# Masks on GpSimd, gelus in place in PSUM and a pair loop in a fixed issue order

## The chip, the cores and the metric

The kernel runs on one core of a Trainium2 chip. The metric is the device time of one execution, in microseconds, and lower is better. Engines are named as the profile names them: PE (TensorE matmuls), DVE (VectorE), ACT (ScalarE), POOL (GpSimd), SP (the queue that issues most transfers). PSUM is the on-chip memory into which the matmuls of this kernel write, SBUF the one that holds its other tiles. A "round" below is one step of the loop over pairs of nodes, normally 128 x 1024 elements.

## The reference, cut to what matters

Two graph layers on 3327 nodes with 64 features. The first is a hyperbolic attention over all pairs of nodes, weighted by an adjacency matrix of zeros and ones. The second sums, for each node, its last hundred neighbours with weights that halve from one to the next, so it needs a count of the later neighbours of each pair.

```python
adj_att = sigmoid(left[:, None] + right[None, :] + b) * adj          # layer 0
support_t = einsum('ij,ijd->id', adj_att, logmap(x[:, None], x[None, :]))
...
mask = (adj != 0)                                                    # layer 1
rank = cumsum(mask, axis=1); deg = rank[:, -1:]
k = minimum(deg, 100); pos = rank - (deg - k)
out = (mask * where(pos > 0, 0.5 ** (k - pos), 0)) @ support + bias
```

## The kernel before

The pair loop goes through four strips of columns (1024, 1024, 768 and 512 wide). Strips 0 to 2 have 26 rounds each; the last handles two row blocks a round and has 13. In each round VectorE makes a mask from the adjacency tile, PE adds it to a running count in PSUM (`pc`), ScalarE or VectorE copies the count out; ScalarE makes a tanh and two gelus, VectorE two large products, and PE sums the result (`po`). Between the rounds of a strip some 90 small VectorE and ScalarE operations finish the strip before (`steps`).

```python
ad = work.tile([P, FMAX], F32, name="ad", bufs=4)                       # adjacency
mask = work.tile([P, FMAX], BF16, name="mask", bufs=3)
V.tensor_scalar(mask[:, :span], ad[:, :span], 0.0, None, op0=ALU.not_equal)
for j in js:
    ...  # T.matmul(pc, ca, before); T.matmul(pc, cb, now)               count
    if j % (2 if b0 == 0 else 4):
        A.activation(kept, pc[:, :F], AF.Relu)                          # count read
    else:
        V.tensor_scalar(kept, pc[:, :F], 0.0, None, op0=ALU.max)
for j in js:
    A.activation(part(sg, j), left_b[:, :F], AF.Tanh, bias=right[:, j : j + 1], scale=0.5)
V.scalar_tensor_tensor(sg, sg, 1.0, ad, op0=ALU.add, op1=ALU.mult)      # first product
pq = ps.tile([P, FMAX], F32, name="pq", bufs=2)                         # pair buffer
...  # four matmuls into pq                                             products
A.activation(s, pq, AF.Gelu, scale=-WG / QS)                            # to SBUF
A.activation(s, s, AF.Gelu, scale=WH)
V.scalar_tensor_tensor(s, s, WD, sg, op0=ALU.add, op1=ALU.mult)         # second product
...  # T.matmul(po, hw, s)                                              total
next(steps, None)
```

The compiler's scheduler may reorder instructions within each engine's queue.

## Time and profile before

| what | before |
|---|---|
| time, median of 3 runs | 460.64 us (459.14 to 461.43) |
| busy PE / DVE / ACT / POOL | 378 / 407 / 369 / 13 us of 459 |
| loop, by the copies that end its strips | 48 to 143.3, 247.3, 330.3 and 390.3 us |
| last stage | 390.3 to 459.1 us |

A busy share says how much of a stretch an engine was occupied. Two more rows of the page, the gelus of the kernel before (operation, shape, count; busy time and mean ns; idle time before them and what ended it):

```profile
L851 ACT ACTIVATE s<-s 128x1024 f32<-128x1024 f32 (+1 forms) x91 | 91.4, 1006 | 0.1
L850 ACT ACTIVATE s<-pq 128x1024 f32<-128x1024 f32 (+1 forms) x91 | 87.7, 969 | 2.6 <-PE pq L848 2.6
```

The first gelu waits for PE only 2.6 us in all: its pair buffer is nearly always ready.

### The profile page before, as it was taken

How to read it: one execution, taken by the hardware profiler on the slowest of the kernel's cores; microseconds unless marked ns; L12 is line 12 of the kernel's file. 1: busy time of each engine (PE TensorE's matmuls, PEld its weight loads, DVE VectorE, ACT ScalarE, POOL GpSimd, SP SyncE). 2: the span in 40 equal slices, each digit the busy share in tenths (PEclk: the TensorE clock that was granted, in tenths of full speed). 3: DMA queues.
4: the chain of work that ended last, by engine and by line, in shares of the span. 5: the costliest groups of instructions: out<-in, count | busy, mean ns of one | idle time of the engine just before them, and what ended most of it. 6: DMA issues, size and time to landing. Idle time of an engine off the chain costs nothing.

```text
span 459.1 us, 4660 instructions
## 1 busy us (share of the span) xinstructions
PE 378.4 (82%) x1484; PEld 153.4 (33%) x1484; DVE 407.1 (89%) x774; ACT 369.2 (80%) x423; POOL 13.3 (3%) x30
## 2 busy tenths in 40 slices
PE   0266699999989799999997999889778897699293
PEld 0035233333323233333333444434322332244152
DVE  3895689999988999999998999999999998999821
ACT  1445989999894999999995999999599995888310
POOL 6000000000000000001000000020000000000000
PEclk9997699999999999999999999999999998899877
DMA  7103354545541444444442444344533420000003
GB/s 201 62 1 72 105 168 143 141 151 163 167 135 46 133 143 140 137 137 137 137 127 75 136 137 140 106 128 125 168 93 111 121 89 1 1 1 1 0 0 82
DMA packets 22840, 47.77 MB, mean 104 GB/s; under 512 B 8652, under 2 KB 9082, under 8 KB 22808
## 3 DMA queue, kind: packets, MB, share of 16 engines
q1 hardware_dynamic: 20522, 46.47, 34.7%
q10 hardware_dynamic: 2062, 0.87, 0.9%
q0 software_dynamic: 224, 0.07, 0.3%
q8 instruction: 13, 0.21, 0.2%
q14 instruction: 19, 0.16, 0.1%
HBM read 45.22 MB, written 0.85 MB: 100 GB/s over the span
## 4 chain that ended last, share of the span: by engine, by line

## 5 line engine op out<-in xcount | busy, mean ns | idle before, releaser
L855 PE MATMUL po<-s,hw 128*65 128x512 f32 (+1 forms) x364 | 165.3, 576 | 11.5 <-DVE s L852 11.1
L842 DVE SCALAR_TENSOR_TENSOR sg<-sg,ad 128x1024 f32<-128x1024 f32 (+1 forms) x91 | 103.5, 1141 | 7.5 <-ACT sg L841 7.3
L852 DVE SCALAR_TENSOR_TENSOR s<-s,sg 128x1024 f32<-128x1024 f32 (+1 forms) x91 | 104.8, 1152 | 3.7 <-ACT s L851 3.6
L841 ACT ACTIVATE sg<-left_b,right 128x1024 f32<-128x1024 f32 (+2 forms) x104 | 102.7, 1001 | 0.1
L851 ACT ACTIVATE s<-s 128x1024 f32<-128x1024 f32 (+1 forms) x91 | 91.4, 1006 | 0.1
L850 ACT ACTIVATE s<-pq 128x1024 f32<-128x1024 f32 (+1 forms) x91 | 87.7, 969 | 2.6 <-PE pq L848 2.6
L829 PE MATMUL pc<-mask,ca 128*128 128x512 bf16 (+1 forms) x175 | 65.7, 375 | 17.3 <-DVE behind_hi L836 7.2
L855 PEld LDWEIGHTS po<-s,hw 128*65 128x65 f32 x364 | 45.2, 138 | 98.9 <-issue 52.7
L847 PE MATMUL pq<-iu,ju 71*128 71x512 f16 (+1 forms) x182 | 67.8, 374 | 11.6 <-ACT s L850 11.6
L830 PE MATMUL pc<-mask,cb 128*128 128x512 bf16 (+1 forms) x182 | 66.7, 376 | 5.3 <-DVE mask L824 5.1
L848 PE MATMUL pq<-iz,jz 128*128 128x512 f16 (+1 forms) x182 | 66.6, 371 | 0.0
L824 DVE TENSOR_SCALAR mask<-ad 128x1024 bf16<-128x1024 f32 (+1 forms) x91 | 59.3, 654 | 3.4 <-PE pc L829 1.8
L894 PE MATMUL pw<-wt,s 128*128 128x512 bf16 (+1 forms) x182 | 41.0, 390 | 12.9 <-DVE s L782 9.2
L834 ACT ACTIVATE behind_hi<-pc 128x1024 uint8<-128x1024 f32 (+2 forms) x37 | 31.8, 860 | 24.3 <-PE pc L830 24.1
L830 PEld LDWEIGHTS <-cb 128*128 128x128 bf16 x182 | 17.9, 99 | 57.8 <-issue 46.6
L834 ACT ACTIVATE behind_lo<-pc 128x1024 uint8<-128x1024 f32 (+2 forms) x33 | 28.2, 853 | 7.1 <-PE pc L830 6.4
L894 PEld LDWEIGHTS <-s 128*128 128x128 f16 x182 | 18.7, 103 | 35.0 <-DVE s L782 9.6
L848 PEld LDWEIGHTS <-jz 128*128 128x128 f16 x182 | 18.1, 99 | 31.5 <-issue 15.3
L829 PEld LDWEIGHTS <-ca 128*128 128x128 bf16 x175 | 17.5, 100 | 30.8 <-issue 19.5
L847 PEld LDWEIGHTS <-ju 71*128 71x128 f16 x182 | 18.1, 100 | 21.4 <-issue 4.8
L836 DVE TENSOR_SCALAR behind_lo<-pc 128x1024 uint8<-128x1024 f32 (+2 forms) x19 | 19.9, 1050 | 1.1 <-PE pc L830 1.1
L771 POOL TENSOR_TENSOR x_sb<-x_sb,bias_b 128x512 f32<-128x512 f32 (+2 forms) x4 | 6.3, 1577 | 418.4 <-DVE w L769 418.4
(209 smaller groups left out, 290.0 us busy)
## 6 DMA issues: line engine op xcount, KB each, us to landing
ad<-in_adj_t SPq DMA_DIRECT2D x65, 512.0 KB, 3.7
ad<-in_adj_t SPq DMA_DIRECT2D x26, 384.0 KB, 3.3
out<-o SPq DMA_DIRECT2D x6, 128.0 KB, 2.0
x_sb<-in_x SPq DMA_DIRECT2D x1, 416.0 KB
x_sb<-in_x ACTq DMA_DIRECT2D x1, 416.0 KB, 6.9
iz<-jz ACTq DMA_DIRECT2D x2, 128.0 KB
iz<-jz SPq DMA_DIRECT2D x2, 128.0 KB, 2.4
iz<-jz SPq DMA_DIRECT2D x2, 96.0 KB
```

The costliest lines, as they stand in the source:

```text
L829: T.matmul(pc[:, f0:f1], ca, before[:, f0:f1], start=False, stop=True, skip_group_check=True)
L830: T.matmul(pc[:, f0:f1], cb, now[:, f0:f1], start=False, stop=True, skip_group_check=True)
L834: A.activation(kept, pc[:, :F], AF.Relu)
L841: A.activation(part(sg, j), left_b[:, :F], AF.Tanh, bias=right[:, j : j + 1], scale=0.5)
L842: V.scalar_tensor_tensor(sg[:, :span], sg[:, :span], 1.0, ad[:, :span], op0=ALU.add, op1=ALU.mult)
L847: T.matmul(part(pq, j, f0, f1), ju[:KB, j, :], iuf[:, f0:f1], start=True, stop=False)
L848: T.matmul(part(pq, j, f0, f1), jz[:, j, :], izf[:, f0:f1], start=False, stop=True)
L850: A.activation(s[:, :span], pq[:, :span], AF.Gelu, scale=-WG / QS)
L851: A.activation(s[:, :span], s[:, :span], AF.Gelu, scale=WH)
L852: V.scalar_tensor_tensor(s[:, :span], s[:, :span], WD, sg[:, :span], op0=ALU.add, op1=ALU.mult)
L855: T.matmul(po[: D + 1, f0:f1], hw[:, j, :], part(s, j, f0, f1), start=j == NB - 1, stop=j == 0)
L894: T.matmul(pw[n], s2[:, j].rearrange("p c d -> p (c d)"), wt[:, f0:f1].bitcast(BF16), start=j == 0, stop=j == NB - 1)
```

## The change

Its intent is to take the masks from the fullest engine, to let the second product have only one SBUF input so that a mask on GpSimd can run beside it, and to write the loop as a software pipeline whose order on PE, VectorE and ScalarE is fixed. Cut to its core:

```diff
+AHEAD = 3
+ON_ACT = ((1, 6), (2, 5), (1, 2), (1, 2))       # share of count reads on ScalarE, by strip
...
+    def edges(n):
+        mask_of[n] = mask = work.tile([P, FMAX], BF16, name="mask", bufs=3)
+        made = G.tensor_scalar(mask[:, : span(n)], ad_of[n][:, : span(n)], 0.0, 0.0,
+                               op0=ALU.is_equal, op1=ALU.is_equal)
+        if n - AHEAD in sg_inst:                # released by the first product of n - 3
+            tc.add_manual_dep(made.ins, sg_inst[n - AHEAD].ins.name, ...)
...
+    with tc.manual_schedule(engines={DVE, Activation, PE}):
...      # for each round n, m = n + 3:
+            total(n - 1)
+            A.activation(pq[:, :w], pq[:, :w], AF.Gelu, scale=-WG / QS)
+            A.activation(pq[:, :w], pq[:, :w], AF.Gelu, scale=WH)
+            sg_inst[n] = V.scalar_tensor_tensor(sg, sg, 1.0, ad_of.pop(n), ...)   # first product
+            read()                              # VectorE's count read, round m - 1
+            edges(m)
+            if two: count(m, js(m)[0])          # last strip only; may read on ScalarE
+            products(n + 1); sigmoids(n + 1)
+            for _ in js(n): next(steps, None)
+            read()
+            count(m, js(m)[-1])                 # may read on ScalarE
+            V.scalar_tensor_tensor(sg, pq, WD, sg, ...)                           # second product
```

Besides, the count no longer starts from a rank-one matmul, later strips fetch `left_b` from memory instead of by transposes, strip changes are pipelined, and the range check's transposes move to the last stage.

More of the change, by code (lines that the diff above doesn't have):

```diff
@@ L31 @@
 JH = 13
+AHEAD = 3
+SGB = 4
+ON_ACT = ((1, 6), (2, 5), (1, 2), (1, 2))
 GSTRIPS = [(0, 7), (7, 7), (14, 6), (20, 6)]
@@ L67 @@
 HS = 1024.0
-CNT = 127.0
 def halves(n):
@@ L480, in fast @@
                     pattern=[[-1, P]], channel_multiplier=1)
-    G.affine_select(out=cb, in_=cb, compare_op=ALU.not_equal, fill=CNT, base=0,
+    G.affine_select(out=cb, in_=cb, compare_op=ALU.not_equal, fill=float(MAX_NEIGH), base=0,
                     pattern=[[-1, P]], channel_multiplier=1)
     G.tensor_sub(ca, ca, cb)
-    row1 = const.tile([1, P], BF16, name="row1")
-    G.memset(row1, 1.0)
-    rowc = const.tile([1, 512], BF16, name="rowc")
-    G.memset(rowc, MAX_NEIGH - CNT)
     node = const.tile([P, NB], F32, name="node")
@@ L526, in fast @@
     s2 = const.tile([P, NB, 2, D], F16, name="s2")
+    left_d = tc.dram_tile([NP], F32, name="left_d")
     post_pool = ctx.enter_context(tc.tile_pool(name="post", bufs=1))
@@ L636, in fast @@
         V.tensor_scalar(right, right, batt, 0.5, op0=ALU.add, op1=ALU.mult)
+        plt = ps.tile([P, P], F32, name="po")
+        T.transpose(plt[:NB, :], left, ident)
+        left_t = const.tile([NB, P], F32, name="left_t")
+        V.tensor_copy(left_t, plt[:NB, :])
+        nc.sync.dma_start(left_d.rearrange("(b p) -> b p", p=P), left_t)
         wn, opx = small("wn"), small("opx")
@@ L658, in behind, with range_steps @@
         return behind_lo[:, j] if j < JH else behind_hi[:, j - JH]
-    def in_range():
-        st = post_pool.tile([P, 4], F32, name="st")
+    def range_steps():
         t1 = post_pool.tile([P, NB], F32, name="st1")
@@ L665, in in_range @@
         V.tensor_reduce(st[:, 0:1], t1, AX.X, ALU.max)
+        yield
         V.scalar_tensor_tensor(t1, x2, c_c, t1, op0=ALU.mult, op1=ALU.mult)
         V.tensor_reduce(st[:, 1:2], t1, AX.X, ALU.max)
+        yield
         V.tensor_mul(t1, bal, node)
         V.tensor_reduce(st[:, 2:3], t1, AX.X, ALU.max)
+        yield
         V.tensor_reduce(st[:, 3:4], t1, AX.X, ALU.min)
         V.tensor_scalar(st[:, 3:4], st[:, 3:4], -1.0, None, op0=ALU.mult)
-        pf = ps.tile([P, P], F32, name="pq", bufs=2)
+    def in_range(pool):
+        pf = pool.tile([P, P], F32, name="pf")
         T.transpose(pf[:4, :], st, ident)
@@ L675, in in_range @@
         V.tensor_reduce(st2, pf[:4, :], AX.X, ALU.max)
-        pf = ps.tile([P, P], F32, name="pq", bufs=2)
+        pf = pool.tile([P, P], F32, name="pf")
         T.transpose(pf[:1, :4], st2, ident[:4, :4])
@@ L782, in post, with strip_in @@
         V.tensor_sub(s2[:, bs, 1], w, s2[:, bs, 0])
-    steps = iter(())
-    for b0, nb in STRIPS:
-        F = nb * P
-        i0 = b0 * P
-        hv = halves(F)
+    rounds = []
+    for k, (b0, nb) in enumerate(STRIPS):
+        per = FMAX // (nb * P)
+        rounds += [(k, max(hi - per, 0), hi) for hi in range(NB, 0, -per)]
+    R = len(rounds)
+    class Strip:
+        pass
+    strips = [Strip() for _ in STRIPS]
+    ad_of, mask_of, sg_of, pq_of, sg_inst = {}, {}, {}, {}, {}
+    reads = []
+    st = const.tile([P, 4], F32, name="st")
+    def strip_in(k):
+        S = strips[k]
+        b0, nb = STRIPS[k]
+        S.F, S.i0, S.hv, S.read, S.before, S.first = nb * P, b0 * P, halves(nb * P), 0, None, True
         blocks = slice(b0, b0 + nb)
-        queue = nc.scalar if b0 == 0 else nc.sync
+        queue = nc.scalar if k == 0 else nc.sync
         iz = strip.tile([P, 8, P], F16, name="iz")[:, :nb]
@@ L798, in fast @@
         queue.dma_start(iz[D:], jz[:D, blocks])
-        izf, iuf = iz.rearrange("p b q -> p (b q)"), iu.rearrange("p b q -> p (b q)")
-        pc = ps.tile([P, FMAX], F32, name="pc")
-        po = ps.tile([P, FMAX], F32, name="po")
-        pl = ps.tile([P, FMAX], F32, name="pq", bufs=2)
-        for b in range(nb):
-            T.transpose(pl[:, b * P : (b + 1) * P], left[:, b0 + b : b0 + b + 1].to_broadcast([P, P]), ident)
-        left_b = strip.tile([P, FMAX], F32, name="left_b", bufs=1)
-        A.copy(left_b[:, :F], pl[:, :F])
@@ L807, in fast @@
-        for f0, f1 in hv:
-            T.matmul(pc[:, f0:f1], row1, rowc[:, : f1 - f0], start=True, stop=True, skip_group_check=True)
-        per = FMAX // F
-        before = None
-        for hi in range(NB, 0, -per):
-            lo = max(hi - per, 0)
-            js = range(hi - 1, lo - 1, -1)
-            span = (hi - lo) * F
-            def part(t, j, a=0, b=F):
-                return t[:, (j - lo) * F + a : (j - lo) * F + b]
-            ad = work.tile([P, FMAX], F32, name="ad", bufs=4)
-            nc.sync.dma_start(ad[:, :span].rearrange("p (b f) -> p b f", f=F),
-                              adj_t[lo * P : hi * P, i0 : i0 + F].rearrange("(b p) f -> p b f", p=P))
-            mask = work.tile([P, FMAX], BF16, name="mask", bufs=3)
-            V.tensor_scalar(mask[:, :span], ad[:, :span], 0.0, None, op0=ALU.not_equal)
-            for j in js:
-                now = part(mask, j)
-                for f0, f1 in hv:
-                    if before is not None:
-                        T.matmul(pc[:, f0:f1], ca, before[:, f0:f1], start=False, stop=True, skip_group_check=True)
-                    T.matmul(pc[:, f0:f1], cb, now[:, f0:f1], start=False, stop=True, skip_group_check=True)
-                before = now
-                kept = behind(j)[:, i0 : i0 + F]
-                if j % (2 if b0 == 0 else 4):
-                    A.activation(kept, pc[:, :F], AF.Relu)
-                else:
-                    V.tensor_scalar(kept, pc[:, :F], 0.0, None, op0=ALU.max)
-            sg = work.tile([P, FMAX], F32, name="sg", bufs=3)
-            for j in js:
-                A.activation(part(sg, j), left_b[:, :F], AF.Tanh, bias=right[:, j : j + 1], scale=0.5)
-            V.scalar_tensor_tensor(sg[:, :span], sg[:, :span], 1.0, ad[:, :span], op0=ALU.add, op1=ALU.mult)
-            pq = ps.tile([P, FMAX], F32, name="pq", bufs=2)
-            for j in js:
-                for f0, f1 in hv:
-                    T.matmul(part(pq, j, f0, f1), ju[:KB, j, :], iuf[:, f0:f1], start=True, stop=False)
-                    T.matmul(part(pq, j, f0, f1), jz[:, j, :], izf[:, f0:f1], start=False, stop=True)
-            s = work.tile([P, FMAX], F32, name="s", bufs=3)
-            A.activation(s[:, :span], pq[:, :span], AF.Gelu, scale=-WG / QS)
-            A.activation(s[:, :span], s[:, :span], AF.Gelu, scale=WH)
-            V.scalar_tensor_tensor(s[:, :span], s[:, :span], WD, sg[:, :span], op0=ALU.add, op1=ALU.mult)
-            for j in js:
-                for f0, f1 in hv:
-                    T.matmul(po[: D + 1, f0:f1], hw[:, j, :], part(s, j, f0, f1), start=j == NB - 1, stop=j == 0)
-                next(steps, None)
@@ L857, in fast @@
-        for _ in steps:
-            pass
-        ot = work.tile([P, FMAX], F32, name="s", bufs=3)[: D + 1]
-        V.tensor_copy(ot[:, :F], po[: D + 1, :F])
-        pa = ps.tile([P, FMAX], F32, name="pq", bufs=2)
+        S.iz, S.iu = iz.rearrange("p b q -> p (b q)"), iu.rearrange("p b q -> p (b q)")
+        S.left = strip.tile([P, FMAX], F32, name="left_b")
+        if k == 0:
+            pl = ps.tile([P, FMAX], F32, name="pq", bufs=2)
+            for b in range(nb):
+                T.transpose(pl[:, b * P : (b + 1) * P], left[:, b0 + b : b0 + b + 1].to_broadcast([P, P]), ident)
+            A.copy(S.left[:, : S.F], pl[:, : S.F])
+        else:
+            nc.sync.dma_start(S.left[:, : S.F], bass.AP(tensor=left_d.tensor, offset=left_d.offset + S.i0,
+                                                         ap=[[0, P], [1, S.F]]))
@@ new lines, in part, with span, js, load @@
+    def part(n, t, j, a=0, b=None):
+        k, lo, hi = rounds[n]
+        F = strips[k].F
+        return t[:, (j - lo) * F + a : (j - lo) * F + (F if b is None else b)]
+    def span(n):
+        k, lo, hi = rounds[n]
+        return (hi - lo) * strips[k].F
+    def js(n):
+        k, lo, hi = rounds[n]
+        return range(hi - 1, lo - 1, -1)
+    def load(n):
+        k, lo, hi = rounds[n]
+        S = strips[k]
+        ad_of[n] = ad = work.tile([P, FMAX], F32, name="ad", bufs=AHEAD + 3)
+        nc.sync.dma_start(ad[:, : span(n)].rearrange("p (b f) -> p b f", f=S.F),
+                          adj_t[lo * P : hi * P, S.i0 : S.i0 + S.F].rearrange("(b p) f -> p b f", p=P))
@@ new lines, in edges, with count @@
+    def edges(n):
[3 more added lines that the diff above has]
+        if n - AHEAD in sg_inst:
+            tc.add_manual_dep(made.ins, sg_inst[n - AHEAD].ins.name,
+                              mybir.DependencyInfo(mybir.DependencyClass.Sync, mybir.DependencyReason.DATA))
+    def count(n, j):
+        k = rounds[n][0]
+        S = strips[k]
+        if S.first:
+            S.pc = ps.tile([P, FMAX], F32, name="pc")
+        now = part(n, mask_of[n], j)
+        for f0, f1 in S.hv:
+            if S.before is not None:
+                T.matmul(S.pc[:, f0:f1], ca, S.before[:, f0:f1], start=False, stop=True, skip_group_check=True)
+            T.matmul(S.pc[:, f0:f1], cb, now[:, f0:f1], start=S.first, stop=True, skip_group_check=True)
+        S.before, S.first = now, False
+        kept = behind(j)[:, S.i0 : S.i0 + S.F]
+        num, den = ON_ACT[k]
+        on_act = S.read % den < num
+        S.read += 1
+        if on_act:
+            A.activation(kept, S.pc[:, : S.F], AF.Relu)
+        else:
+            reads.append((kept, S.pc[:, : S.F]))
@@ new lines, in read, with sigmoids, products @@
+    def read():
+        while reads:
+            kept, pc = reads.pop(0)
+            V.tensor_scalar(kept, pc, 0.0, None, op0=ALU.max)
+    def sigmoids(n):
+        S = strips[rounds[n][0]]
+        sg_of[n] = sg = work.tile([P, FMAX], F32, name="sg", bufs=SGB)
+        for j in js(n):
+            A.activation(part(n, sg, j), S.left[:, : S.F], AF.Tanh, bias=right[:, j : j + 1], scale=0.5)
+    def products(n):
+        S = strips[rounds[n][0]]
+        pq_of[n] = pq = ps.tile([P, FMAX], F32, name="pq", bufs=2)
+        for j in js(n):
+            for f0, f1 in S.hv:
+                T.matmul(part(n, pq, j, f0, f1), ju[:KB, j, :], S.iu[:, f0:f1], start=True, stop=False)
+                T.matmul(part(n, pq, j, f0, f1), jz[:, j, :], S.iz[:, f0:f1], start=False, stop=True)
@@ new lines, in total, with strip_out @@
+    def total(n):
+        k, lo, hi = rounds[n]
+        S = strips[k]
+        if hi == NB:
+            S.po = ps.tile([P, FMAX], F32, name="po")
+        for j in js(n):
+            for f0, f1 in S.hv:
+                T.matmul(S.po[: D + 1, f0:f1], hw[:, j, :], part(n, s_of[n], j, f0, f1),
+                         start=j == NB - 1, stop=j == 0)
+    def strip_out(k):
+        S = strips[k]
+        S.ot = work.tile([P, FMAX], F32, name="sg", bufs=SGB)[: D + 1]
+        V.tensor_copy(S.ot[:, : S.F], S.po[: D + 1, : S.F])
@@ L863, in fast, with strip_out2 @@
+    def strip_out2(k):
+        S = strips[k]
+        b0, nb = STRIPS[k]
+        pa = ps.tile([P, FMAX], F32, name="po")
         for b in range(nb):
             c0 = (b // 4) * 512 + (b % 4) * (D + 1)
-            T.transpose(pa[:, c0 : c0 + D + 1], ot[:, b * P : (b + 1) * P], ident[: D + 1, : D + 1])
+            T.transpose(pa[:, c0 : c0 + D + 1], S.ot[:, b * P : (b + 1) * P], ident[: D + 1, : D + 1])
         agg = post_pool.tile([P, 8, D + 1], F32, name="agg", bufs=2)
         for c in range(0, nb, 4):
-            n = min(4, nb - c)
@@ L869, in fast @@
-            A.copy(agg[:, c : c + n], pa[:, c * P : c * P + n * (D + 1)].rearrange("p (b d) -> p b d", b=n))
-        steps = post(agg[:, :nb], b0, nb)
-        if b0 == 0:
-            in_range()
+            m = min(4, nb - c)
+            A.copy(agg[:, c : c + m], pa[:, c * P : c * P + m * (D + 1)].rearrange("p (b d) -> p b d", b=m))
+        return post(agg[:, :nb], b0, nb)
+    s_of = {}
+    steps = range_steps()
+    strip_in(0)
+    for n in range(AHEAD + 1):
+        load(n)
+    for n in range(AHEAD):
+        edges(n)
+        for j in js(n):
+            count(n, j)
+            read()
@@ new lines, in fast @@
+    tc_order = tc.manual_schedule(engines={mybir.EngineType.DVE, mybir.EngineType.Activation, mybir.EngineType.PE})
+    with tc_order:
+        products(0)
+        sigmoids(0)
+        late_total = None
+        for n in range(R):
+            k, lo, hi = rounds[n]
+            S = strips[k]
+            new, second = hi == NB and k > 0, n and rounds[n - 1][2] == NB and k > 0
+            m = n + AHEAD
+            if m + 1 < R:
+                if rounds[m + 1][2] == NB:
+                    strip_in(rounds[m + 1][0])
+                load(m + 1)
+            if second:
+                steps = strip_out2(k - 1)
+            elif n:
+                total(n - 1)
+            pq, w = pq_of.pop(n), span(n)
+            A.activation(pq[:, :w], pq[:, :w], AF.Gelu, scale=-WG / QS)
+            A.activation(pq[:, :w], pq[:, :w], AF.Gelu, scale=WH)
+            sg = sg_of[n]
+            sg_inst[n] = V.scalar_tensor_tensor(sg[:, :w], sg[:, :w], 1.0, ad_of.pop(n)[:, :w],
+                                                op0=ALU.add, op1=ALU.mult)
+            if new:
+                strip_out(k - 1)
+            read()
+            if m < R:
+                edges(m)
+            two = m < R and len(js(m)) == 2
+            if two:
+                count(m, js(m)[0])
+            if n + 1 < R:
+                products(n + 1)
+                sigmoids(n + 1)
+            for _ in js(n):
+                next(steps, None)
+            if lo == 0:
+                for _ in steps:
+                    pass
+            read()
+            if m < R:
+                count(m, js(m)[-1])
+            s_of[n] = sg
+            V.scalar_tensor_tensor(sg[:, :w], pq[:, :w], WD, sg[:, :w], op0=ALU.add, op1=ALU.mult)
+            if second:
+                total(n - 1)
+        total(R - 1)
+        strip_out(len(STRIPS) - 1)
+        steps = strip_out2(len(STRIPS) - 1)
@@ L902, in fast @@
                 next(steps, None)
+            if j == 10:
+                in_range(l1_ps)
         for _ in steps:
```

## The prediction

> **What bounds the kernel now.** The kernel has three parts: a prologue on node statistics (to about 46 us), a loop over pairs of nodes in four column strips (to about 390 us), and the weighted sum of the second layer. The change lives in the loop, so I read the page's busy shares first, then a table by strip, then one round in order of time. The chain of waits is empty for this run, so the bound has to be worked out from loads. The page:
>
> ```profile
> PE 378.4 (82%) x1484; PEld 153.4 (33%) x1484; DVE 407.1 (89%) x774; ACT 369.2 (80%) x423; POOL 13.3 (3%) x30
> ...
> DVE  3895689999988999999998999999999998999821
> ...
> L842 DVE SCALAR_TENSOR_TENSOR sg<-sg,ad 128x1024 f32<-128x1024 f32 (+1 forms) x91 | 103.5, 1141 | 7.5 <-ACT sg L841 7.3
> L852 DVE SCALAR_TENSOR_TENSOR s<-s,sg 128x1024 f32<-128x1024 f32 (+1 forms) x91 | 104.8, 1152 | 3.7 <-ACT s L851 3.6
> ...
> L824 DVE TENSOR_SCALAR mask<-ad 128x1024 bf16<-128x1024 f32 (+1 forms) x91 | 59.3, 654 | 3.4 <-PE pc L829 1.8
> ```
>
> VectorE is the fullest engine and its two large products hardly wait. GpSimd is empty. The busy time of each engine by strip (columns: stretch, its length, PE, weight loads, VectorE, ScalarE, GpSimd, clock, DMA share, GB/s):
>
> ```profile
> 48.00:143.20 95.20, 90.00 (x289) 31.77 (x288) 87.73 (x88) 86.47 (x89) 0.00 (x0) 0.96 0.50 147
> 143.20:246.50 103.30, 95.64 (x330) 34.16 (x330) 101.03 (x176) 97.18 (x105) 2.19 (x1) 1.00 0.45 130
> 246.50:329.30 82.80, 73.40 (x324) 33.59 (x323) 80.35 (x165) 76.83 (x105) 2.40 (x1) 1.00 0.44 125
> 329.30:390.30 61.00, 52.25 (x170) 17.79 (x168) 57.48 (x129) 52.61 (x78) 1.00 (x1) 0.97 0.29 85
> ```
>
> In strips 1 to 3 VectorE is busy 94 to 98% of the time: it is the bound there. In strip 0 (no small per-strip work yet) PE leads with 90.0 of 95.2. The three engines stand within 10% of each other, so relieving one soon meets the next. Costs of one round of 1024 columns, from start to next start, are in this stretch of the timeline:
>
> ```profile
> 228.91 0.69 DVE L824 TENSOR_SCALAR mask<-ad 128x1024 bf16<-128x1024 f32 x1
> 229.36 1.01 ACT L850 ACTIVATE s<-pq 128x1024 f32<-128x1024 f32 x1
> 229.52 0.16 DVE L512 SCALAR_TENSOR_TENSOR rn<-rs_t,rn 128x8 f32<-128x8 f32 x1
> 229.53 0.38 PE L829 MATMUL pc<-mask,ca 128*128 128x512 bf16 x1
> 229.59 1.22 DVE L852 SCALAR_TENSOR_TENSOR s<-s,sg 128x1024 f32<-128x1024 f32 x1
> 229.75 0.38 PE L830 MATMUL pc<-mask,cb 128*128 128x512 bf16 x1
> ...
> 230.26 1.15 ACT L841 ACTIVATE sg<-left_b,right 128x1024 f32<-128x1024 f32 x1
> ...
> 230.80 1.22 DVE L836 TENSOR_SCALAR behind_lo<-pc 128x1024 uint8<-128x1024 f32 x1
> 230.87 1.93 PE L855 MATMUL po<-s,hw 128*65 128x512 f32 x4
> 231.30 1.05 ACT L851 ACTIVATE s<-s 128x1024 f32<-128x1024 f32 x1
> ...
> 232.25 1.02 ACT L850 ACTIVATE s<-pq 128x1024 f32<-128x1024 f32 x1
> ...
> 232.64 0.38 PE L829 MATMUL pc<-mask,ca 128*128 128x512 bf16 x1
> ```
>
> Read as spacings: mask 0.61 us, a large VectorE product 1.14, a VectorE read of the count 1.14; first gelu 0.90, tanh 1.04, second gelu 0.95, a ScalarE read of the count about 0.92 (its 1.02 less the usual overlap); a 16-bit matmul 0.22, the four fp32 pieces of a total 1.77. A PE round is 8 x 0.217 + 1.77 = 3.50 us.
>
> **What the Trainium skill says.** "SBUF — State Buffer", Who interferes with whom: a VectorE instruction with two SBUF inputs contends with a GpSimd instruction that reads SBUF; one with at most one SBUF input (outside the two-port modes) does not. The trace agrees on the contention: GpSimd's add of 128x512 took 2.19 us beside VectorE work, that of 128x256 only 0.73, and a mask then took 1.18 us against 0.69.
>
> ```profile
> 215.55 2.19 POOL L771 TENSOR_TENSOR x_sb<-x_sb,bias_b 128x512 f32<-128x512 f32 x1 [207.49 <-DVE w L769]
> ...
> 217.11 1.18 DVE L824 TENSOR_SCALAR mask<-ad 128x1024 bf16<-128x1024 f32 x1
> ```
>
> "GPSIMD Engine Reference", Elementwise and Performance pitfalls: a light one-input body takes 1.03 cycles per element at 1.2 GHz, a compare body that is not unrolled 2.03. No large one-input GpSimd operation is in the trace; its 128x128 cast took 0.31 us. With about 0.15 us fixed (its one-element memsets), my estimate for a 128x1024 mask is 1.0 to 1.9 us. "ScalarE: Activation LUTs", Step-by-step: an activation that writes PSUM is quicker than one that writes SBUF. No activation here writes PSUM, so this is open; reading PSUM (first gelu 1.02) is a little under reading SBUF (second 1.05).
>
> **The change part by part.** (1) The masks leave VectorE: 65 x 0.61 + 26 x 0.47 = 52 us, of which some 3 us lie in the prologue. (2) Count reads move from ScalarE to VectorE. Shares on ScalarE were 1/2, 3/4, 3/4, 3/4; they become 1/6, 2/5, 1/2, 1/2. VectorE gains 26 x 0.33 x 1.14 = 9.9, 26 x 0.35 x 1.14 = 10.4, 26 x 0.25 x 0.87 = 5.7 and 26 x 0.25 x 0.61 = 4.0, together 30 us; ScalarE is relieved of about 25. So VectorE loses a net 22 us. (3) Gelus in place in PSUM: the second product then has one PSUM and one SBUF input, so it does not fight the mask. The product itself stays one element per cycle. The price is that a pair buffer stays held until that product has read it, with two buffers in all. (4) The fixed order: PE does total(n-1), products(n+1), count(n+3); the mask for n+3 is released by the first product of n, so it should run under the count read and the second product, a window of 2 x 1.14 = 2.3 us. (5) Strip changes are pipelined: now PE makes no total from 142.8 to 153.3 us, perhaps 4 us lost, and about as much at the two others. (6) The range check's transposes go from the first strip change to the last stage, about +1.5 us there (eight small VectorE operations and two round trips).
>
> Loads by strip after the change. Strip 0: PE 26 x 3.50 = 91, VectorE 26 x (2.28 + 0.95) = 84, ScalarE 26 x 3.04 = 79. PE bounds it; with the cold start 93, from 95.2. Strip 1: VectorE 26 x (2.28 + 0.68) = 77, plus the copy of 1.1, plus the small per-strip steps, about 15 us (the rest of the 101 us now); 93. PE 91, ScalarE 88. Strip 2 (768 columns): VectorE 26 x 2.18 + 16 = 73, PE 26 x 2.64 = 69, ScalarE 72. Strip 3: 13 rounds, PE 45.5, VectorE 52, ScalarE 50.
>
> On top comes the order of work. Where a count is read by ScalarE, that read stands in front of the next gelus, and a ring closes over two rounds: read 0.92, two gelus 1.85, second product 1.14, one PE round 3.50, some 0.3 of hand-over, 7.7 us, or 3.85 a round. For strip 1, two rounds in five are so: 10 x 0.35 = 3 us more, 96. For strip 2 every second round is: 0.72 + 1.46 + 0.87 + 2.64 + 0.3 = 6.0, 3.0 a round, 78. In strip 3 the ScalarE read comes before the tanh and the ring is not closed; 53, plus 2 for the drain, 55. Sum 93 + 96 + 78 + 55 = 322 against 342.3: 20 us. Prologue: five masks and some reads leave a busy VectorE, about -2. Gelus in PSUM, if quicker, -1. Last stage +1.5. Small two-input steps that meet a mask in strips 1 to 3, +2. In all -19.5, so 441; as my ring may be kinder than I count, I put 440.
>
> **The rivals.** First, GpSimd becomes the bound. If a mask takes well over 2.3 us, or is stopped by VectorE, each first product waits, or the count does, in every round. For it: the 2.19 us add. Against: the placement avoids just those neighbours. At 2.6 us a mask, 0.3 us x 84 round-equivalents = 25 us, and the time would be 460 to 465. Second, PE becomes the only bound and the order is perfect: 91 + 92 + 72 + 50 = 305, a gain of 37, 423 us. For it: all three loads then fit under or near PE's. Against: in-order queues with handshakes each round seldom close without gaps, and the ring above. Third, the fixed order stalls: PE's count waits on the mask while the next total's data are ready, or the two held pair buffers starve PE. Half a microsecond a round is 42 us, cancelling the gain: about 465. DMA is no rival, at half share in every strip.
>
> **Range and chances.** The middle of the loads and ring is 440. The good end is the second rival, 423 to 425. The bad end takes half of the losses of the first or third, about 453. A gain of over 2% needs under 451.4: chance 0.84. Within 2%: 0.12. Slower than 469.9: 0.04.
>
> **What would show it.** Right: GpSimd busy 90 to 170 us, masks of 1.0 to 1.9 us that lie under the count read and the second product; VectorE busy about 385 in all; the first product still near 1.22 us; PE over 93% in strip 0; strips of about 93, 96, 78 and 55 us; gaps at strip changes gone. Wrong: first products or steps stretched by tenths beside masks, counts that wait for GpSimd, or gelus that wait for PE in most rounds. If strip 2 runs below 2.9 us a round, my ring is wrong.

## The result, and the profile after

The changed kernel took 581.9 us, median of 4 runs (580.9 to 583.2), against 461.0: a ratio of 1.262, interval 1.255 to 1.269. All ratios here are the mean time of one kernel's runs over that of the other's of the same rounds, so not quite the ratio of the medians that stand beside them. Executions over 1.5% slower than the fastest of the same kernel are left out of the means. Results are correct. The page of the kernel after:

```profile
PE 404.8 (70%) x1442; PEld 162.0 (28%) x1460; DVE 411.1 (71%) x712; ACT 356.2 (62%) x392; POOL 320.5 (55%) x119
...
L857 POOL TENSOR_SCALAR mask<-ad 128x1024 bf16<-128x1024 f32 (+1 forms) x91 | 309.2, 3402 | 172.6 <-DVE sg L966 104.5
...
L874 PE MATMUL pc<-mask,cb 128*128 128x512 bf16 (+1 forms) x179 | 67.5, 388 | 107.0 <-POOL mask L857 106.2
L988 DVE SCALAR_TENSOR_TENSOR sg<-pq,sg 128x1024 f32<-128x1024 f32 (+1 forms) x91 | 104.0, 1143 | 53.7 <-ACT pq L964 53.7
L966 DVE SCALAR_TENSOR_TENSOR sg<-sg,ad 128x1024 f32<-128x1024 f32 (+1 forms) x91 | 103.7, 1140 | 32.7 <-ACT sg L895 32.7
```

No engine is above 71% now: nobody is full, everybody waits. A mask takes 3.4 us on average, 3.63 at full width, where I had estimated 1.0 to 1.9. PE waited 106 us for masks, and GpSimd waited 104 us for first products: two engines that wait for each other are a ring. The products themselves kept their length (1.14 us on average as before), so GpSimd does not slow them here; the small steps are another matter, to which e11_pool_free_order comes back. By strip, in the columns of the prediction:

```profile
48.00:170.05 122.05, 98.67 (x301) 35.31 (x306) 83.91 (x81) 87.90 (x88) 95.15 (x27) 0.93 0.40 119
170.05:298.59 128.54, 98.28 (x314) 35.48 (x318) 102.62 (x151) 90.07 (x96) 95.00 (x28) 0.96 0.36 105
298.59:413.05 114.46, 82.02 (x318) 35.80 (x318) 83.24 (x149) 75.37 (x101) 74.99 (x27) 0.93 0.34 95
413.05:511.11 98.06, 60.48 (x144) 18.74 (x145) 61.08 (x122) 46.95 (x66) 37.23 (x11) 0.77 0.13 38
```

The strips lost 27, 25, 31 and 38 us (122.05 against 143.25 - 48 = 95.25, and so on); the last stage, 68.1 us, lost nothing. In strip 0 the ring can be followed in the timeline (start us, length us, engine and line; in brackets the idle time before and what ended it):

```profile
99.98 7.22 POOL L857 TENSOR_SCALAR mask<-ad 128x1024 bf16<-128x1024 f32 x2 [1.49 <-DVE sg L966]
...
103.66 0.38 PE L874 MATMUL pc<-mask,cb 128*128 128x512 bf16 x1 [1.50 <-POOL mask L857]
...
104.51 1.23 DVE L888 TENSOR_SCALAR behind_lo<-pc 128x1024 uint8<-128x1024 f32 x1 [1.37 <-PE pc L874]
...
105.65 1.22 DVE L988 SCALAR_TENSOR_TENSOR sg<-pq,sg 128x1024 f32<-128x1024 f32 x1
...
106.78 1.22 DVE L966 SCALAR_TENSOR_TENSOR sg<-sg,ad 128x1024 f32<-128x1024 f32 x1
...
108.24 7.22 POOL L857 TENSOR_SCALAR mask<-ad 128x1024 bf16<-128x1024 f32 x2 [1.03 <-PE pc L874]
...
116.49 7.22 POOL L857 TENSOR_SCALAR mask<-ad 128x1024 bf16<-128x1024 f32 x2 [1.03 <-PE pc L874]
126.68 7.22 POOL L857 TENSOR_SCALAR mask<-ad 128x1024 bf16<-128x1024 f32 x2 [2.96 <-DVE sg L966]
```

The first row holds two masks. The first of them is done at 103.6; PE's count follows at 103.66; VectorE has waited 1.37 us for it before its count read at 104.51; then come, in the fixed order, the second product and the first product, whose end at 108.00 releases the next mask at 108.24. (The row at 108.24 names PE's count, which ended about as late, at 108.07. I take the product: the program makes the mask wait for it, and the mask at 99.98, whose row names the product, also starts 0.24 us after the product's end.) The ring is 108.24 - 99.98 = 8.26 us long and holds two rounds, so 4.13 us a round, where PE needs 3.50. This is not yet the whole loss of the strip, which takes 122.05 / 26 = 4.69 us a round: every sixth round ScalarE reads the count in front of its gelus, and the same pair of rounds then takes 126.68 - 116.49 = 10.19 us. In the last strip the ring closes within one round:

```profile
405.97 3.63 POOL L857 TENSOR_SCALAR mask<-ad 128x1024 bf16<-128x1024 f32 x1 [3.33 <-DVE sg L966]
...
409.65 0.38 PE L874 MATMUL pc<-mask,cb 128*128 128x512 bf16 x1 [1.39 <-POOL mask L857]
...
410.06 0.60 ACT L881 ACTIVATE behind_hi<-pc 128x512 uint8<-128x512 f32 x1 [3.80 <-PE pc L874]
...
411.91 1.23 DVE L966 SCALAR_TENSOR_TENSOR sg<-sg,ad 128x1024 f32<-128x1024 f32 x1 [4.66 <-ACT sg L895]
...
413.38 3.63 POOL L857 TENSOR_SCALAR mask<-ad 128x1024 bf16<-128x1024 f32 x1 [3.78 <-DVE sg L966]
```

The mask holds the count, the count holds ScalarE's read, that read stands in front of the next tanh, the tanh holds the first product, and the first product releases the next mask: 7.41 us here, and 7.4 to 7.6 in seven of the ten rounds from this one on. The other three take 9.6 to 11.2 us: in them VectorE stands in a block of small steps, or waits in one for ScalarE, before it comes to the first product. PE is busy for only 60.48 of the strip's 98.06 us, and its granted clock is 0.77 there, against 0.97 before.

### The profile page after: what moved, and what is told of

Its sections match the earlier page's. It is cut to its first block, busy times and chain, and to the rows that moved or that the text cites. A ratio compares the mean times of both kernels' runs of the same rounds, so it can differ in the third digit from the quotient of the medians.

```text
span 579.2 us, 4867 instructions
## 1 busy us (share of the span) xinstructions
PE 404.8 (70%) x1442; PEld 162.0 (28%) x1460; DVE 411.1 (71%) x712; ACT 356.2 (62%) x392; POOL 320.5 (55%) x119
## 4 chain that ended last, share of the span: by engine, by line
## 5 line engine op out<-in xcount | busy, mean ns | idle before, releaser
L857 POOL TENSOR_SCALAR mask<-ad 128x1024 bf16<-128x1024 f32 (+1 forms) x91 | 309.2, 3402 | 172.6 <-DVE sg L966 104.5
L912 PE MATMUL po<-sg,hw 128*65 128x512 f32 (+1 forms) x364 | 184.1, 635 | 21.7 <-DVE sg L988 21.2
L988 DVE SCALAR_TENSOR_TENSOR sg<-pq,sg 128x1024 f32<-128x1024 f32 (+1 forms) x91 | 104.0, 1143 | 53.7 <-ACT pq L964 53.7
L963 ACT ACTIVATE pq<-pq 128x1024 f32<-128x1024 f32 (+1 forms) x91 | 86.7, 953 | 29.5 <-PE pq L903 29.2
L964 ACT ACTIVATE pq<-pq 128x1024 f32<-128x1024 f32 (+1 forms) x91 | 86.2, 947 | 2.9
L912 PEld LDWEIGHTS po<-sg,hw 128*65 128x65 f32 x364 | 52.4, 150 | 107.6 <-issue 65.1
L902 PE MATMUL pq<-iu,ju 71*128 71x512 f16 (+1 forms) x182 | 71.0, 390 | 0.1
L881 ACT ACTIVATE behind_hi<-pc 128x1024 uint8<-128x1024 f32 (+2 forms) x23 | 19.0, 827 | 53.9 <-PE pc L874 53.9
L881 ACT ACTIVATE behind_lo<-pc 128x1024 uint8<-128x1024 f32 (+2 forms) x19 | 15.6, 822 | 55.4 <-PE pc L874 55.4
L888 DVE TENSOR_SCALAR behind_lo<-pc 128x1024 uint8<-128x1024 f32 (+2 forms) x33 | 34.7, 1052 | 11.7 <-PE pc L874 11.4
L888 DVE TENSOR_SCALAR behind_hi<-pc 128x1024 uint8<-128x1024 f32 (+2 forms) x29 | 30.6, 1054 | 10.7 <-PE pc L874 10.7
```

The costliest lines, as they stand in the source:

```text
L857: made = G.tensor_scalar(mask[:, : span(n)], ad_of[n][:, : span(n)], 0.0, 0.0, op0=ALU.is_equal, op1=ALU.is_equal)
L888: V.tensor_scalar(kept, pc, 0.0, None, op0=ALU.max)
L902: T.matmul(part(n, pq, j, f0, f1), ju[:KB, j, :], S.iu[:, f0:f1], start=True, stop=False)
L912: T.matmul(S.po[: D + 1, f0:f1], hw[:, j, :], part(n, s_of[n], j, f0, f1), start=j == NB - 1, stop=j == 0)
L963: A.activation(pq[:, :w], pq[:, :w], AF.Gelu, scale=-WG / QS)
L964: A.activation(pq[:, :w], pq[:, :w], AF.Gelu, scale=WH)
```

## The experiments

Theory A: the 3.63 us mask, its release and the fixed order form the ring, and the time goes with the mask's length. Rival B: the fixed order, or pair buffers held through the gelus, costs by itself. Rival C: GpSimd and VectorE hinder each other at SBUF. Eighteen kernels ran, each timed in three rounds beside the kernel before (medians of 459.8 to 461.7 us in the sets). "No mask" kernels let PE read the upper half of each fp32 adjacency element as a 16-bit number, which is right for zeros and ones, as the inputs are, and not for other weights.

**The mask in the changed order.**

```diff
 e1_mask_vector
-        made = G.tensor_scalar(mask, ad, 0.0, 0.0, op0=ALU.is_equal, op1=ALU.is_equal)
-        (release)
+        V.tensor_scalar(mask, ad, 0.0, None, op0=ALU.not_equal)
 e2_mask_one_op
-        made = G.tensor_scalar(mask, ad, 0.0, 0.0, op0=ALU.is_equal, op1=ALU.is_equal)
+        made = G.tensor_scalar(mask, ad, 0.0, None, op0=ALU.is_gt)
 e3_mask_cast
+        made = G.tensor_copy(mask, ad)
 e4_no_mask
-        mask, made, release
+        mask_of[n] = ad_of[n].bitcast(BF16).rearrange("p (f two) -> p f two", two=2)[:, :, 1]
```

> The changed kernel with its masks made on VectorE again (one comparison, placed where GpSimd's mask stood, no release); all else of the change stays. Theory A (the 3.63 us GpSimd mask stands in a ring: first product, mask, count matmuls, count read, second product, next first product): the ring loses its longest link, time 440 to 475 us, last strip under 65 us. Rival B (the fixed order with two pair buffers held through the gelus is what costs): 540 us or more.

> The mask stays on GpSimd but with one comparison (greater than zero) in place of two. If the length of a mask goes with the number of its operations: about 1.9 to 2.7 us instead of 3.63, and by theory A about 450 to 500 us. If it does not: about 3.6 us and 580. Rival B: 540 or more whatever the mask takes.

> The mask is a plain cast on GpSimd (the same values, as adjacency is 0 or 1). From the 128x128 cast of 0.29 us less 0.13 fixed I expect 1.4 us; theory A then 435 to 455 us, rival B 540 or more. Rival C (GpSimd and VectorE hinder one another whenever both read SBUF): first products stretched beyond 1.3 us and time above 470.

> No mask at all: the count matmuls read the upper 16 bits of each fp32 adjacency element as bf16 (right for 0 and 1). Fixed order and gelus in PSUM stay. Theory A: 420 to 440 us, which is what the rest of the change is worth. Rival B: 540 or more. If the count matmuls are slowed by the 4-byte stride, each is over 0.22 us from start to start.

| kernel | mask, 128x1024 | time, us | ratio to before |
|---|---|---|---|
| changed | 3.63 us on GpSimd | 581.9 | 1.262 |
| e2_mask_one_op | 2.77 us on GpSimd | 544.2 | 1.182 |
| e1_mask_vector | 0.68 us on VectorE | 524.4 | 1.138 |
| e3_mask_cast | 1.04 us on GpSimd | 501.4 | 1.089 |
| e4_no_mask | none | 494.1 | 1.074 |

The groups of masks of the one-comparison kernel, then of the cast kernel:

```profile
L857 POOL TENSOR_SCALAR mask<-ad 128x1024 bf16<-128x1024 f32 x65 | 180.7, 2780 | 159.5 <-DVE sg L965 99.1 <-DVE st L668 29.7 <-PE pc L873 10.5
```

```profile
L857 POOL CAST mask<-ad 128x1024 bf16<-128x1024 f32 x65 | 68.6, 1056 | 239.2 <-DVE sg L965 173.7 <-DVE st L668 32.8 <-PE po L911 11.7
```

The time follows the mask's length, as A says: the ring loses 2.6 us with the cast, is then by estimate 8.26 - 2.6 = 5.7 us for two rounds, below PE's 7.0, and only 7 us remain above having no mask. e1_mask_vector stands outside this row: its mask is short, but it stands in VectorE's own fixed queue and costs 524 - 494 = 30 us there. Rival C's sign is absent: beside the cast, first products took 1.22 us. Nor does the strided read of the kernels without a mask slow the counts: they follow one another by 0.22 to 0.23 us in e4_no_mask, by 0.22 before. The mask costs 582 - 494 = 88 us in this order. But every one of the four times missed my ranges, all of them upwards by 44 us or more, and without any mask the kernel is still 7.4% slower than before. A alone is not enough; it falls as the only cause. Nor is B as I had put it (540 or more). A second, separate cost of some 50 us was left to find.

**The other parts, one at a time.**

```diff
 e7_before_psum (kernel before)
-            A.activation(s, pq, AF.Gelu, scale=-WG / QS); A.activation(s, s, AF.Gelu, scale=WH)
-            V.scalar_tensor_tensor(s, s, WD, sg, ...)
+            A.activation(pq, pq, AF.Gelu, scale=-WG / QS); A.activation(pq, pq, AF.Gelu, scale=WH)
+            V.scalar_tensor_tensor(s, pq, WD, sg, ...)
 e8_before_no_mask (kernel before)
-            V.tensor_scalar(mask[:, :span], ad[:, :span], 0.0, None, op0=ALU.not_equal)
+            mask = upper halves of ad
 e9_no_mask_free_order (e4_no_mask)
-    tc_order = tc.manual_schedule(engines={DVE, Activation, PE})
+    tc_order = ExitStack()
 e10_act_read_later (e4_no_mask)
-            A.activation(kept, pc, AF.Relu)      # at once, in front of the next gelus
+            act_reads.append((kept, pc))         # issued behind the two gelus of the next round
```

> The kernel before with one part of the change: both gelus in place in PSUM, so that the second product reads PSUM and a pair buffer stays held until then. Rival B in its narrow form (two held pair buffers starve PE): 470 us or more. If it is harmless or the gelus gain 0.05 us each: 453 to 463.

> The kernel before with no mask at all (counts read the upper half of the adjacency elements), its own order kept. VectorE is relieved of 59 us and PE at 3.5 us a round becomes the bound: 420 to 440 us. This is the partner of the run without masks in the changed order (494 us): the gap between the two is the cost of everything in the change but the mask.

> The changed kernel without masks, and without the fixed issue order: the compiler's scheduler may reorder within each engine. If the fixed order is what costs the 34 us that remain without masks: 425 to 450. If it is the gelus in PSUM or the shifted count reads: still 480 to 500.

> The changed kernel without masks, fixed order kept, but each count read on ScalarE moved behind the next round's two gelus instead of in front of them. The ring that I named in the prediction then opens in some 27 rounds of the first three strips, by 0.7 to 1.0 us each: 470 to 482 us. If that ring isn't what costs: 488 to 497.

e7_before_psum: three of its six runs are slow and left out; the fast ones took 513.3, 517.1 and 519.8 us, a mean of 516.7 against 461.5, ratio 1.120 (the median of all six is 520.7, its ratio 1.129). In the order of before, gelus in PSUM are harmful, and a row of its list of waits (engine and line, what it waited for: total us, times, longest) says how:

```profile
ACT pq L850 <- PE pq L848: 46.8, 36, 3.6
```

The first gelu now waits 46.8 us for its pair buffer instead of 2.6. A buffer that used to be free after the first gelu is held until the second product, and there are only two.

e8_before_no_mask took 456.0 us, ratio 0.987 (0.981 to 0.993). This is the sharpest contradiction to my reading. VectorE's busy time fell from 407 to 366 us, and the time by 1.3%. Its strip 1, in the columns of the strip tables, was no shorter (105.28 against 103.30 us in the prediction's row):

```profile
141.85:247.13 105.28, 99.50 (x335) 35.16 (x335) 90.35 (x149) 97.95 (x106) 2.20 (x1) 0.98 0.45 136
```

VectorE went from 98% to 86% busy there and PE stayed at 93 to 95%. VectorE was busy, but not the bound: to take work from it alone shortened nothing in that order. What paced the strip instead is not shown; PE and ScalarE (97.95 us busy) were nearly as full.

e9_no_mask_free_order took 444.4 us, ratio 0.963: with the scheduler free and no mask, the rest of the change is a gain. The fixed order costs 494 - 444 = 50 us. e10_act_read_later took 484.7 us, 9.4 less than e4_no_mask, somewhat below the 12 to 24 expected: the ring through ScalarE's count reads exists and is about a fifth of the 50.

**The ring cut elsewhere.**

```diff
 e11_pool_free_order (changed kernel)
-    tc_order = tc.manual_schedule(...)
+    tc_order = ExitStack()
 e5_no_release (changed kernel)
-        if n - AHEAD in sg_inst: tc.add_manual_dep(...)
 e1b_vector_free_order (e1_mask_vector)
-    tc_order = tc.manual_schedule(...)
+    tc_order = ExitStack()
 e6_before_pool (kernel before)
-            V.tensor_scalar(mask, ad, 0.0, None, op0=ALU.not_equal)
+            G.tensor_scalar(mask, ad, 0.0, 0.0, op0=ALU.is_equal, op1=ALU.is_equal)
```

> The changed kernel with the GpSimd mask of two comparisons and its release kept, but without the fixed issue order. If the long mask costs only through the in-order ring: GpSimd's 309 us fit beside the loop, 450 to 480 us. If GpSimd's own length or the release bounds it: 500 to 540.

> The changed kernel, fixed order, without the release of a mask by the first product. The ring is cut at that link and masks can run ahead by up to two rounds. If the ring is the cause and VectorE and GpSimd hardly hinder one another: rounds of about 3.7 us, 505 to 530. If a two-input product is stopped by a mask that reads SBUF (rival C): first products stretched to 2 us and more, 550 to 620.

> Masks on VectorE and no fixed order, the rest of the change kept (gelus in PSUM, count shares, pipelined emission). From the run without masks in free order (444 us) plus the masks' 52 us on a VectorE that has about 40 us of slack in the loop: 452 to 468 us. If VectorE is the bound one to one: 480 or more.

> The kernel before with one part of the change: masks on GpSimd with two comparisons, no release, the scheduler's own order. GpSimd has 309 us of masks for a loop of 342: if it neither waits nor hinders VectorE, 455 to 475 us. If the masks hinder VectorE's two-input products, or stand in the way of counts: 500 to 560, with products stretched in the first case and PE waiting for masks in the second.

e11_pool_free_order: 483.4 us, ratio 1.047, just above its first range. The same long mask costs 88 us with the fixed order and 483 - 444 = 39 without it. GpSimd runs all 27 masks of strip 0 back to back in 97.09 us, yet that strip is only 1.3 us longer than without masks (e9_no_mask_free_order). The 39 us lie in strips 1 to 3 (18, 11 and 9 us), where the small steps run. There a cost shows that I had overlooked: VectorE is busy 409.7 us against 383.1, and the large products are 4 us of that. Most of the rest are small steps with two SBUF inputs, stretched beside the masks; this group took 0.16 us each without masks:

```profile
L509 DVE TENSOR_TENSOR rs_t<-rs_t,rs_g 128x8 f32<-128x8 f32 x18 | 7.2, 402 | 0.1
```

How the 39 us divide between GpSimd's pace and these stretched steps was not separated.

e5_no_release: 516.1 us, ratio 1.117, inside the range for a cut ring: 66 us are won by cutting that one link, though masks are as long as ever. Its profile fell in a slow run (524 us), so I read from it only what the mean lengths of operations say:

```profile
L963 DVE SCALAR_TENSOR_TENSOR sg<-sg,ad 128x1024 f32<-128x1024 f32 x65 | 97.7, 1502 | 14.7 <-ACT sg L892 14.7
L985 DVE SCALAR_TENSOR_TENSOR sg<-pq,sg 128x1024 f32<-128x1024 f32 x65 | 79.0, 1215 | 19.3 <-ACT pq L961 19.3
```

Without the release the first product (two SBUF inputs) is stretched from 1.22 to 1.50 us, the second (one input in PSUM) not at all. So rival C is real, some 0.28 x 65 = 18 us of VectorE's busy time, and it is what the release was made to avoid; but the release cost more than that. e6_before_pool agrees in kind: 499.2 us, ratio 1.082; there both products have two SBUF inputs and both were stretched, to 1.34 and 1.40 us, the masks to 3.94. It fell between my two ranges. e1b_vector_free_order: 473.0 us, ratio 1.024 (1.018 to 1.031), 5 us above its range. A mask on VectorE thus costs 473 - 444 = 29 us in the new emission (the order in which the changed program writes its instructions down) and only 5.5 in the kernel before. That the new one has VectorE nearer to its limit (383 of 443 us even without masks) would explain it; that is argued, not shown.

**Which queue the fixed order hurts.** These six ran after the first twelve, to settle the 50 us. All are without masks.

```diff
-    manual_schedule(engines={DVE, Activation, PE})
+    manual_schedule(engines={DVE})              # e12_fix_vector
+    manual_schedule(engines={PE})               # e13_fix_pe
+    manual_schedule(engines={Activation})       # e14_fix_scalar
 e15_free_shares (e9_no_mask_free_order)
-ON_ACT = ((1, 6), (2, 5), (1, 2), (1, 2))
+ON_ACT = ((1, 2), (3, 4), (3, 4), (3, 4))
 e16_free_sbuf (e9_no_mask_free_order)
+            s = work.tile([P, FMAX], F32, name="s", bufs=2)
-            gelus in place in pq; second product reads pq
+            gelus into s; second product reads s
 e17_fixed_interleaved (e10_act_read_later)
-            a block of small steps in each round
+            single small operations: one after the first product, two after the
+            count read, one after the second product (twice that in the last strip)
```

> No mask, order fixed on VectorE only, free on PE and ScalarE. If the cost of the fixed order is VectorE running the small per-strip steps and the second product strictly in turn (chains of small operations with nothing large between them): 475 to 495. If it is another queue: 444 to 455.

> No mask, order fixed on PE only. If PE's turn (total before products before count) starves the gelus: 470 to 495. If not: 442 to 455.

> No mask, order fixed on ScalarE only. The count reads then stand in front of the gelus. From the 9 us that moving them back gained in the fixed order: 450 to 465. If the small squares and copies of the steps, waiting at ScalarE's head for VectorE, are the main cost: 470 to 495.

> No mask, free order, count reads shared as in the kernel before (half, then three quarters on ScalarE). VectorE loses 30 us and ScalarE gains 25. If VectorE at 383 us of 443 still bounds: 430 to 440. If PE bounds: 440 to 448. If ScalarE becomes the bound: 450 or more.

> No mask, free order, both gelus written to SBUF as in the kernel before. If holding a pair buffer until the second product costs time here too: 430 to 440. If the pipelined emission hides it: 443 to 450, the gelus being 0.03 to 0.06 us longer each.

> No mask, order fixed on all three queues, ScalarE's count reads behind the gelus (484.7 us so far), and the small per-strip steps split to single operations that stand between the large ones of VectorE. If blocks of small dependent operations are what VectorE's fixed order costs: 450 to 468 us, last strip under 62 us. If not: 478 or more.

| kernel | order fixed on | time, us | ratio to before |
|---|---|---|---|
| e4_no_mask | all three | 494.1 | 1.074 |
| e10_act_read_later | all three | 484.7 | 1.051 |
| e17_fixed_interleaved | all three | 463.8 | 1.005 |
| e12_fix_vector | VectorE | 475.1 | 1.029 |
| e14_fix_scalar | ScalarE | 475.2 | 1.029 |
| e13_fix_pe | PE | 446.5 | 0.967 |
| e9_no_mask_free_order | none | 444.4 | 0.963 |
| e15_free_shares | none | 448.8 | 0.971 |
| e16_free_sbuf | none | 433.0 | 0.940 |

PE's order is as good as free. VectorE's and ScalarE's cost 31 us each, and together not the sum (50). e12_fix_vector lies at the edge of the range that I gave for VectorE's small steps (475 to 495); e14_fix_scalar lies in its second range (470 to 495), the one for ScalarE's small squares and copies that wait at the head of its queue. That was not taken further: of ScalarE's waits in its trace, 12.5 and 9.3 us are for counts, 10.7 and 8.9 for small steps. In the timeline of the kernel with VectorE fixed, one block of steps in the last strip shows what happens:

```profile
354.86 0.16 DVE L504 TENSOR_SCALAR rs_t<-t 128x6 int32<-128x6 int32 x1
355.05 0.17 DVE L505 TENSOR_SCALAR rn<-rs_t 128x6 int32<-128x6 int32 x1
...
359.81 0.23 DVE L741 SCALAR_TENSOR_TENSOR k<-k,absr,rn 128x6 f32<-128x6 f32 x1 [2.23 <-ACT k L739]
...
362.40 1.22 DVE L983 SCALAR_TENSOR_TENSOR sg<-pq,sg 128x1024 f32<-128x1024 f32 x1
```

From 354.86 to 362.40 VectorE does nothing but tiny operations on 128x6 elements, each about 0.2 us after the one it depends on, and 2.23 us of that is a wait for ScalarE's tanh of a 128x6 tile. The second product, for which PE waits 4.27 us, stands behind them. In the kernel before, the scheduler put each of these between two large operations, where one costs 0.07 us from its start to the next start (228.84 to 228.91 and 229.52 to 229.59 in its timeline). e17_fixed_interleaved does that by hand, in a fixed order: 463.8 us, 21 less than e10_act_read_later, within the range, though its last strip (394.65 - 328.08 = 66.6 us) stayed above the 62 that I had named. So of the 50 us, 9 are the ScalarE reads in front of the gelus and 21 the blocks of small steps; about 20 are left, from 463.8 to 444.4. By the strips of the two traces they lie in strips 1, 2 and 3 (7, 3 and 14 us), none in strip 0; what causes them stays open.

e16_free_sbuf is the best version: 433.0 us, ratio 0.940 (0.934 to 0.946). Writing the gelus to SBUF again wins 11 us over the same kernel in PSUM, so holding the pair buffers costs even in the pipelined emission: the first gelu waits 9.3 us for its pair buffer's products there and 2.1 here. e15_free_shares (448.8 us, between its ranges) says that the new shares of the count reads are worth 4 us. Both hold for an adjacency of zeros and ones only.

## Why the prediction was wrong

I forecast 440 us, range 425 to 453, with 0.04 on slower. It was 582.

**The step that failed first: "my estimate for a 128x1024 mask is 1.0 to 1.9 us".** It was 3.63. I had the rival in hand ("GpSimd becomes the bound") and the right threshold (2.3 us), but took a mask's length from a page's figures for loop bodies, none of them for this instruction, and from a cast of 128 columns. The cast indeed costs 1.04 us; the two comparisons cost 2.6 more. This is the first of two steps that made the forecast fail, 88 us of the 142 between 440 and 582; the other is the fixed order, below.

**The size of that rival.** I charged the excess over 2.3 us to each round: 25 us for 2.6. For the measured lengths the same rule gives (3.63 - 2.3) x 84 = 112 us, where the mask cost 88, and (2.77 - 2.3) x 84 = 39, where the one comparison cost 544 - 494 = 50. So the rule was of the right size and its input was not. Its path was incomplete: the cost comes from a ring of mask, count, count read, second product and first product. My own prediction traced a ring through ScalarE's reads and did not look for one through the release that the change adds.

**"VectorE ... is the bound there."** e8_before_no_mask refutes it for the kernel before: taking all masks away gains 1.3%. In the new emission the same masks are worth 29 us (e1b to e9). So what relief of VectorE is worth depends on the order around it, and a share of 98% does not tell. That the scheduler fills VectorE's gaps with early work would explain it; that is my reading, not shown.

**The fixed order.** Named as the third rival, "half a microsecond a round is 42 us", and given little weight. It is 50 us without masks, in VectorE's and ScalarE's queues. PE's own order costs 2 us (e13), so the PE stall that I described is not these 50; with the masks on GpSimd half of it came true, as counts waited 106 us for masks.

**The gelus in PSUM, "if quicker, -1".** They are quicker: 1.013 and 1.008 us at full width against 1.030 and 1.068. Yet they cost 11 us (e9 to e16) or 55 (e7), because of the held buffer, which I mentioned as "the price" and then left out of the sum.

**"Small two-input steps that meet a mask ..., +2".** In e11_pool_free_order VectorE was busy 27 us longer than without masks, most of it for these steps.

**What held.** The ScalarE ring exists: I counted 3 + 5 us for strips 1 and 2, and moving the reads gave 9.4. That the sums agree is partly luck: by strip it gave 4.8, 3.3 and 1.7 us, half of it in strip 0, where I had counted none. The release does protect products (1.22 us kept, 1.50 without). The last stage is as long as before. And the loads by strip were about right for a kernel without the mask and the fixed order: the strips of e9_no_mask_free_order took 96.8, 95.3, 79.3 and 52.5 us, where I had 93, 96, 78 and 55. Luck has a part in that: my numbers hold some 8 us for a ring of the fixed order, which e9 does not have, and e9 holds about 11 for the buffers, which I left out. With the gelus in SBUF (e16_free_sbuf) the strips took 93.7, 92.3, 72.8 and 49.0 us, close to the 91, 92, 72 and 50 of my second rival. I had priced a schedule that the change does not have.

The causes do not add up to single shares: taking away the mask first gives 88 + 50, taking away the fixed order first gives 99 + 39, from 582 to 444 either way. About 49 us exist only where both are present.

## What to carry to other kernels

Before work is moved to another engine, time that very operation there at its full size, and draw the ring that its new waits close: what it waits for, who waits for it, and how many rounds the ring holds. A high busy share under a free scheduler is a hint, not a bound: remove the work in an experiment that may be wrong in its result but not in its shape, and see what the time does. When an order is fixed by hand, small dependent operations belong one by one between large ones, and nothing that waits for another engine belongs in front of what the slowest engine needs next.

## What the Trainium skill lacked or had wrong

- "GPSIMD Engine Reference", Elementwise and Performance pitfalls: it has figures for loop bodies and none for a comparison instruction, which is dearer than they suggest. A 128x1024 mask from fp32 to a 16-bit type took 2.77 us with one comparison and 3.63 with two, so 0.86 us (about one cycle an element at the page's 1.2 GHz) for the second and far more for the first: a cast of the same tile took 1.04. With 0.15 us fixed, estimated from its one-element memsets, these are 3.1, 4.1 and 1.04 cycles an element, against 1.03 for a light body and 2.03 for a compare body on the page. The cast agrees; the comparisons don't.
- "SBUF — State Buffer", Who interferes with whom: confirmed in kind, with a size that the page does not give. Beside free-running masks products with two SBUF inputs went from 1.22 to 1.34 and 1.40 us on average (e6; 1.50 in e5, a slow run), one with a PSUM and an SBUF input stayed at 1.22 (e5), and a group of 128x8 steps went from 0.16 to 0.40 us (e9, e11).
- "ScalarE: Activation LUTs", Step-by-step: writing PSUM is quicker, as it says, but by 0.02 to 0.06 us on 1.03 to 1.07. Its caveat, that this is of use only if TensorE doesn't need most of PSUM, points at the cost of held buffers but gives no size: 11 to 55 us here.
- No page gives the pace of small VectorE operations that depend on one another (0.2 us each in a row here, 0.07 where one stands between two large ones) or what blocks of them can cost in a fixed order: singling them out won 21 us.
